# A bias copied into PSUM by ScalarE, border rows packed into tiles that run on demand, and new order lists

## The chip, the core and the metric

The kernel runs on one core of a Trainium2 chip. It is one program with five instruction queues: TensorE (PE, matrix products into PSUM), VectorE (DVE), ScalarE (ACT), GpSimd (POOL, which also issues the indirect DMAs) and SyncE (SP, which issues the other DMAs). Each queue runs in order; semaphores join them. The metric is device microseconds of one execution.

## What is computed

The input x has 16 x 512 = 8192 rows (tokens) of 512 float32 values. Each token has a pathway id (0 to 499), an id c (0 to 4) and a mask m (0 or 1, used as an index into a table of three).

```python
h = _ln(x, pw_g[pathway_ids], pw_b[pathway_ids])
h = _ln(h, cp_g[compartment_ids], cp_b[compartment_ids])
t = _ln(x, tm_g[time_steps], tm_b[time_steps])
m = x + _mlp_ln(memory_state, ...)[:, None, :]
n = x + _mlp_ln(noise_state, ...)[:, None, :]
r = x + _mlp_ln(resource_state, ...)[:, None, :]
s = _ln(x, ms_g[scale_type], ms_b[scale_type])
w = jax.nn.softmax(aw)
cat = jnp.concatenate([w[0]*h, w[1]*t, w[2]*m, w[3]*n, w[4]*r, w[5]*s], axis=-1)
return _mlp_ln(cat, int_W1, int_b1, int_W2, int_b2, int_g, int_be)
```

Here `_ln` is a layer norm over the 512 values with a row's own gain and offset, and `_mlp_ln` is a first layer, silu, a second layer and a layer norm. The output is x plus the returned rows. compartment_ids and time_steps are both c, and scale_type is m.

## The kernel before

**Sorting.** t and s depend on a token only through x, c and m. So the kernel first sorts the 8192 tokens by their pair (c, m), 15 groups in a snake order (NG = 15, B = 16 batches), and works through 64 tiles of 128 sorted rows, four to a window, 16 windows. Within a tile of one group the gains of t and s can be folded into the weights: `s_part` (ACT, line 247) and `build` (DVE, line 255) make the matrix `vs` of a group, and only where the group changes from the tile that last used that buffer.

**The border rows.** A tile through which a border between two groups runs is worked with the group of its middle row. The rows on the other side of the border (at most 64 a border) need a correction, and the kernel works these out first as extra tiles: before, one tile for the borders at which m changes, and six in which each half (64 rows) belongs to one of two neighbouring borders of c (NX = 6, lines 1043 to 1313). An extra tile gathers its rows of x (`gx.e`), takes their sums and norm (`xs.e`, `nv.e`), gathers the difference of the two groups' gains (`gr`), multiplies (`mt`, line 1274), transposes on TensorE (`ey`, line 1281), copies out (`ez`, line 1288), multiplies by the weights (`ex`, line 1296), gathers and adds a row of the bias table (`ea`, `ee`) and is written to a table in DRAM by SP (`eo`, lines 1309 and 1313). The gathers are always issued. The steps on TensorE, VectorE and ScalarE stand behind a condition, `some[k] > 0`, which says that a border of the tile isn't at the edge of a tile. Later each tile of the main loop gathers one row of that table per token (`ga`, line 165) and adds it to its first layer.

**The main loop.** For each tile the first layer is the sum of three products: x with the weight block X, the normed x with `vs` (V, line 394), and h with block H. X and H of two tiles and two column halves go through a seven-product scheme (`m7`, line 442, 128x256 products). Then come the add (`ha`, line 462), the silu (`hs`, ACT, line 465), a transpose in 32x32 blocks on VectorE (`tz`, line 191) and 16 DMAs on SP (`sZ`, line 199) which finish the transpose. GpSimd makes the sums that the second layer's seven-product scheme needs (`zs`, lines 522 to 528), and TensorE runs it (`q7`, line 545), for window w - 1 while window w's first layer is at work. Each pair of tiles has two PSUM banks for it, `pq_pa` and `pq_pb`; there are eight banks in all. The second layer's bias enters as a product: before products 1 and 5 of each pair, TensorE multiplies a constant with the bias, which `bias_parts` has split into three bf16 parts (line 543, 96x128 with 96x256). ScalarE and VectorE copy and add the halves out of PSUM (`kf`, `ku`, `sf`, `sl`, lines 554 to 574). The last window's second layer is an ordinary product (`l2`, line 477), with its bias added by VectorE (line 605).

**Order.** The program text is three lists of short names. ORDER is the preparation, the extra tiles and window 0's first layer; WINDOW is run for w = 0 to 14, where c, p, n and m stand for windows w, w - 1, w + 1 and w + 2; LAST is the last window. Each name calls a function through the tables at lines 1360 to 1384, and each engine gets its instructions in the order of the list. A queue that waits holds back what stands behind it.

## Time and profile before

| | |
|---|---|
| median of 3 runs | 937.35 us (935.75 to 942.13) |
| the profiled execution | 936.66 us |
| its span, first to last instruction | 934.8 us |
| mean granted TensorE clock | 0.991 |

The profile names an instruction by its line, engine, what it writes and reads, and its shape. A float32 product counts as two records. Busy time of TensorE is that of pipelined instructions, whose own durations overlap: the step from one start to the next is what a product costs in a dense stretch. The chain of work that ended last is followed back from the end, and its pieces don't overlap. In a table by stretches the columns are the length, then for each engine its busy time and number of instructions, then the granted clock, the busy share of the DMA engines and GB/s. A wait's row gives what waited, on what, the total, how often, and the longest.

### The profile page before, as it was taken

Reading aid. Unit: us, or ns where it says so; the run is one execution under the profiler, and the core shown is the slowest. Engines: PE = TensorE matmul, PEld = TensorE weight load, DVE = VectorE, ACT = ScalarE, POOL = GpSimd, SP = SyncE. Lnnn points to the kernel's source line nnn. Section 1 sums busy time; section 2 is a strip of 40 time slices with the busy share of each in tenths; the row PEclk is TensorE's granted clock in tenths of the full one; section 3 lists DMA queues with packets and bytes.
Section 4 is the critical chain, followed back from the end, with each engine's and each line's share of the span. In section 5 each row is a group of like instructions: output and inputs, shape, how many; then the busy total and the mean of one; then the engine's idle time right before and its main releaser. Section 6 shows DMA issues by size and latency. Waiting matters only on the chain. (4 is left out here: it accounts for less than half of the span.)

```text
span 934.8 us, 13620 instructions
## 1 busy us (share of the span) xinstructions
PE 898.4 (96%) x3687; PEld 644.4 (69%) x3687; DVE 746.1 (80%) x1359; ACT 500.9 (54%) x1211; POOL 662.1 (71%) x705
## 2 busy tenths in 40 slices
PE   6979999999999999999999999999999999999995
PEld 6644447868677677878576776778686867777782
DVE  8678677969688798979687886959798987979475
ACT  4688646264635638373645446273747465472322
POOL 9666787767777687687677677767867776875523
PEclk9899999999999999999999999999999999999998
DMA  8667686776767686777767685857767676866512
GB/s 282 215 241 224 206 255 163 213 209 184 235 176 236 171 243 162 226 198 206 212 174 232 183 241 155 250 157 229 205 200 218 182 224 176 249 171 185 166 40 95
DMA packets 88860, 186.66 MB, mean 200 GB/s; under 512 B 24372, under 2 KB 24372, under 8 KB 88780
## 3 DMA queue, kind: packets, MB, share of 16 engines
q0 software_dynamic: 31376, 106.19, 38.8%
q1 hardware_dynamic: 56700, 79.50, 29.5%
q8 instruction: 30, 0.49, 0.2%
q14 instruction: 50, 0.41, 0.1%
q10 hardware_dynamic: 704, 0.08, 0.1%
HBM read 101.78 MB, written 19.94 MB: 130 GB/s over the span
## 5 line engine op out<-in xcount | busy, mean ns | idle before, releaser
L394 PE MATMUL p<-vs,catV 128*128 128x512 f32 x512 | 227.7, 592 | 1.7 <-DVE vs L255 1.5
L394 PEld LDWEIGHTS p<-vs,catV 128*128 128x128 f32 x512 | 97.0, 190 | 106.0 <-issue 97.1
L340 ACT ACTIVATE junk<-pw 128x512 bf16<-128x512 f32 x60 | 37.8, 630 | 170.7 <-DVE pw L337 162.2
L636 POOL DMA_INDIRECT out<-yb,tok x64 | 72.1, 1126 | 57.3 <-DVE yb L632 25.3
L442 PE MATMUL p<-wh__80,catH 128*128 128x256 f32 x480 | 110.9, 379 | 0.0
L442 PEld LDWEIGHTS p<-wh__80,catH 128*128 128x128 f32 x480 | 91.2, 190 | 18.4 <-issue 6.7
L362 POOL TENSOR_TENSOR rsh<-veh,mhalf 128x1 f32<-128x1 f32 x64 | 55.8, 872 | 42.3 <-DVE veh L358 37.1
L165 POOL DMA_INDIRECT pw<-in_pw,i_pw x64 | 66.1, 1032 | 26.9 <-DVE rH L191 9.2
L381 POOL TENSOR_TENSOR xbs<-xbs,rows 128x512 f32<-128x512 f32 x64 | 81.9, 1281 | 1.0
L165 POOL DMA_INDIRECT xbs<-in_x,tok x64 | 66.6, 1041 | 22.2 <-issue 16.5
L165 POOL DMA_INDIRECT cp<-cp_rows,i_cp x64 | 67.6, 1056 | 17.3 <-issue 14.4
L366 ACT ACTIVATE pw<-pw,rsh 128x512 f32<-128x512 f32 x64 | 45.8, 719 | 63.0 <-DVEq L238 43.0
L165 POOL DMA_INDIRECT add<-rows,i_add x64 | 66.9, 1045 | 16.4 <-issue 11.0
L465 ACT ACTIVATE add<-add 128x512 f32<-128x512 f32 x64 | 40.3, 632 | 70.0 <-DVE add L462 67.6
L307 ACT ACTIVATE xm<-xbs,nmx,rsx 128x512 f32<-128x512 f32 x64 | 49.1, 809 | 26.8 <-DVE nmx L301 25.7
L442 PE MATMUL p<-wt,catH 128*128 128x256 f32 x240 | 56.7, 379 | 0.0
L442 PE MATMUL u<-wt,catX 128*128 128x256 f32 x240 | 56.6, 379 | 0.0
L442 PE MATMUL u<-wx__79,ss 128*128 128x256 f32 x240 | 56.5, 379 | 0.0
L191 DVE STREAM_TRANSPOSE rH<-pw 128x512 f32<-128x512 f32 x60 | 41.0, 701 | 18.6 <-ACT pw L366 16.6
L337 DVE SCALAR_TENSOR_TENSOR pw<-pw,rsx 128x512 f32<-128x512 f32 x64 | 53.0, 829 | 2.3
L442 PE MATMUL u<-wt,ss 128*128 128x256 f32 x240 | 54.4, 379 | 0.0
L442 PE MATMUL u<-wx__79,catX 128*128 128x256 f32 x240 | 54.4, 379 | 0.0
(421 smaller groups left out, 2097.9 us busy)
## 6 DMA issues: line engine op xcount, KB each, us to landing
catX<-rX SPq DMA_DIRECT2D x240, 64.0 KB
catV<-rV SPq DMA_DIRECT2D x240, 64.0 KB
catZ<-rZ SPq DMA_DIRECT2D x240, 64.0 KB
catH<-rH SPq DMA_DIRECT2D x240, 64.0 KB
rows<-adde SPq DMA_DIRECT2D x14, 128.0 KB
yb<-in_int_W SPq DMA_DIRECT2D x1, 1024.0 KB
catH<-in_int_W SPq DMA_DIRECT2D x1, 1024.0 KB
w1x<-in_int_W SPq DMA_DIRECT2D x1, 1024.0 KB
```

Source lines behind the costliest of these rows:

```text
L165: nc.gpsimd.indirect_dma_start(dst, None, table, bass.IndirectOffsetOnAxis(ap=idx, axis=0), **kw)
L191: nc.vector.transpose(rot[:, :, :, j, :].rearrange("p q c t -> p c q t"), src.rearrange("p (c q t) -> p c q t", c=NC, q=Q))
L307: nc.scalar.activation(t, st["xb"][:, j, :], AF.Identity, bias=st["nm"][:, j : j + 1], scale=st["rs"][:, j : j + 1])
L337: nc.vector.scalar_tensor_tensor(h, h, st["rs"][:, j : j + 1], pw[:, D:], ALU.mult, ALU.add)
L340: nc.scalar.activation(junk, x, AF.Identity, accum_out=sums[:, 0, k : k + 1])
L362: nc.gpsimd.tensor_tensor(rs, st.pop(("ve", j)), mhalf[:, :1], ALU.pow)
L366: nc.scalar.mul(pw[:, :D], pw[:, :D], st.pop(("rs", j)))
L381: nc.gpsimd.tensor_add(st["xb"][:, j, :], st["xb"][:, j, :], rows[:, 2, :])
L394: nc.tensor.matmul(st["p1", g], st["c" + blk][:, g, c, :], m[:, c, :], start=(blk == first and c == order[0]), stop=(blk == last and c == ...
L442: nc.tensor.matmul(dst, m[:, c], at_["half1"][k][:, c], start=(k == 1 and c == 0), stop=(c == NC - 1), skip_group_check=True)
L465: nc.scalar.activation(st["add", g], st["add", g], AF.Silu)
L636: nc.gpsimd.indirect_dma_start(out_rows[j], bass.IndirectOffsetOnAxis(ap=tok[:, j, w : w + 1], axis=0), yb[:, j, :], None)
```

## The change

1. **The second layer's bias.** The bias products and the three bf16 parts go. `rows` becomes a view of `blocks`, seven half rows, the last of them zero; `bias_parts` only subtracts one half from the other. Two new pieces fill a bank before its products, which then all accumulate: `kb` (`put_bias`) is one ScalarE copy of 128x512 into the bank, [bias half, zeros], in windows 1 to 14, four a window; `kz` (`clear_sums`) is a product of zeros that does the same clearing once in window 0. `weights_back` restores the bias for the last window.
2. **The border rows.** Every border's rows that need work are counted (`count_ends`), and added up in front of each other (`row_places`), so that they fill up to seven full tiles without gaps (NT_ = 7). The tile of m borders takes 64 rows for each of its two borders. Which token a packed row is comes from products with a comparison matrix (`of_begins`, `kinds`) and a new gather of one value a row from the sorted list, which is now also written to DRAM (`in_order`, `gt`). A tile runs when the total reaches it. The gathers of tokens, of x and of the differences now stand behind that condition too, on GpSimd; the gathers of bias rows don't. Each tile is written by one DMA of SP, not two.
3. **The lists.** ORDER, WINDOW and LAST are new throughout. In WINDOW, V's fourth tile (`lV.c.3`) now comes ahead of the first product of Z, and its third (`lV.c.2`) ahead of the last two. In ORDER, the blocks of x's weights (`wk`) are all summed before the first variance (`xe.0`), and the transposes of x come first. In LAST, the last `sh` stands ahead of `po.c.0`, where it stood behind `po.c.1`.

The diff, cut to its core:

```diff
 WINDOW = """
-    ha.p.2 sh.c.1 lV.c.1 lV.c.0 m7.c.0.1 m7.c.1.1 hs.p.2 tz.p.3 tz.p.2 f1.c.2 sp.c.3 fs.c.2 f1.c.3 xs.n.0 fs.c.3
-    gc.c.2 gc.c.3 ga.c.0 sh.c.0 bd.c.3 fv.c.2 f2.c.2 fv.c.3 f2.c.3 sZ.p.0 sZ.p.1 sZ.p.2 sZ.p.3 sp.c.2 q7.p.0.1
-    q7.p.0.2 lV.c.3 fp.c.2 fp.c.3 zs.p.0 fn.c.2 fn.c.3 xs.n.1 xs.n.2 kf.p.0 bd.c.2 th.c.3 th.c.2 zs.p.1 q7.p.1.1
-    q7.p.0.5 q7.p.0.7 xs.n.3 tx.n.3 sf.p.0 tx.n.1 tx.n.0 xe.n gh.n.0 zs.p.2 q7.p.0.6 zs.p.4 zs.p.5 zs.p.3 xp.n
-    q7.p.1.2 kf.p.1 ku.p.0 sf.p.1 vd.n tx.n.2 sl.p.0 r1.c.0 xm.n gc.n.1 zs.p.6 zs.p.7 sh.c.3 q7.p.1.5 q7.p.0.3
-    q7.p.1.7 q7.p.0.4 kf.p.2 nv.n.3 nv.n.1 kf.p.3 sf.p.2 tv.n.3 tv.n.1 sf.p.3 sl.p.1 nv.n.2 nv.n.0 lq.p.0 ga.c.2
-    gc.n.0 ga.c.1 gh.n.1 sH.c.1 sH.c.3 sH.c.0 sH.c.2 q7.p.1.6 q7.p.1.3 q7.p.1.4 lV.c.2 m7.c.1.2 lq.p.1 ku.p.1
...
+    kz.p.2 kz.p.1 ha.p.2 f1.c.2 kb.p.2 kz.p.0 ga.c.2 tz.p.3 lV.c.1 lV.c.0 m7.c.1.1 m7.c.0.1 kb.p.1 sh.c.1 kb.p.0
+    gc.c.2 gc.c.3 sp.c.3 hs.p.2 tz.p.2 bd.c.3 f1.c.3 fs.c.2 sp.c.2 xs.n.0 fs.c.3 fv.c.2 bd.c.2 f2.c.2 fv.c.3
+    f2.c.3 sZ.p.0 sZ.p.1 sZ.p.2 fp.c.2 ga.c.0 zs.p.0 fp.c.3 lV.c.3 q7.p.0.1 q7.p.0.2 q7.p.0.7 xs.n.1 fn.c.2 fn.c.3
+    kf.p.0 xs.n.2 zs.p.1 zs.p.2 q7.p.0.5 q7.p.0.6 ku.p.0 kf.p.1 tx.n.1 th.c.2 th.c.3 tx.n.3 r1.c.0 sZ.p.3 gh.n.0
+    zs.p.3 zs.p.4 sf.p.0 tx.n.2 sf.p.1 zs.p.5 xs.n.3 zs.p.6 q7.p.1.2 vd.n tx.n.0 r1.c.1 xe.n xp.n ga.c.1 ga.c.3
+    sH.c.3 sh.c.2 zs.p.7 sH.c.2 kz.p.3 q7.p.1.1 sl.p.0 sH.c.0 sH.c.1 q7.p.0.3 q7.p.0.4 kb.p.3 kf.p.2 va.n sf.p.2
+    sl.p.1 xm.n q7.p.1.5 q7.p.1.7 nv.n.1 nv.n.3 lq.p.0 kf.p.3 f1.n.0 tv.n.3 tv.n.1 sf.p.3 q7.p.1.6 lV.c.2 q7.p.1.4
...
@@ -207,7 +213,11 @@
     def gather_x(st, js=range(NJ)):
         t, w = st["tok"]
         for j in js:
-            gather(st["xb"][:, j, :], x_rows, t[:, j, w : w + 1])
+            if "n" in st:
+                with tc.If(at_["some", 3][int(st["w"][1]) * Q + j] > 0):
+                    gather(st["xb"][:, j, :], x_rows, t[:, j, w : w + 1])
+            else:
+                gather(st["xb"][:, j, :], x_rows, t[:, j, w : w + 1])
 
     def gather_h(st, j):
...
     def weights_back():
         nc.gpsimd.tensor_add(w2[:, :2, D // 2 :], w2[:, :2, D // 2 :], w2[:, :2, : D // 2])
+        nc.gpsimd.tensor_add(blocks[:, 1], blocks[:, 1], blocks[:, 0])
 
     def bias_parts():
-        BF16 = mybir.dt.bfloat16
         H = D // 2
-        parts = 96
...
+        nc.gpsimd.memset(blocks[:, 6], 0.0)
+        nc.vector.tensor_sub(blocks[:, 1], blocks[:, 1], blocks[:, 0])
+
+    def clear_sums(st, i):
+
+        if st["w"] == 0:
+            st["pq", i] = psum(f"pq0_{i // 2}{'ab'[i % 2]}").rearrange("p (k n) -> p k n", k=2)
+            zero = blocks[:, 6].bitcast(mybir.dt.bfloat16)
+            nc.tensor.matmul(st["pq", i].rearrange("p k n -> p (k n)"), zero[:, :P], zero, start=True, stop=True,
+                             skip_group_check=True)
+
+    def put_bias(st, i):
+        if st["w"]:
+            st["pq", i] = psum(f"pq{st['w']}_{i // 2}{'ab'[i % 2]}").rearrange("p (k n) -> p k n", k=2)
+        nc.scalar.copy(st["pq", i], blocks[:, 1::5] if i % 2 else blocks[:, 0::6])
 
...
     def seventh(st, p, k):
-        ab, ed = sums_of(st, p)
-        home = {1: ab[:, 0], 6: ab[:, 0], 2: ab[:, 1], 5: ed[:, 0], 3: ed[:, 0], 7: ed[:, 1], 4: ed[:, 1]}[k]
+        i, half = {1: (0, 0), 6: (0, 0), 2: (0, 1), 5: (1, 0), 3: (1, 0), 7: (1, 1), 4: (1, 1)}[k]
         if ("zp", p) not in st:
             st["zp", p] = {1: st["cZ"][:, 2 * p, :2], 2: st["cZ"][:, 2 * p, 2:]}
-        bias = at_["bias"]
-        if k in bias:
-            nc.tensor.matmul(home, at_["share"], bias[k], start=True, stop=False, skip_group_check=True)
         for c in range(2):
-            nc.tensor.matmul(home, st["zp", p][k][:, c], at_["half"][k][:, c], start=False, stop=(c == 1),
-                             skip_group_check=True)
+            nc.tensor.matmul(st["pq", 2 * p + i][:, half], st["zp", p][k][:, c], at_["half"][k][:, c], start=False,
+                             stop=(c == 1), skip_group_check=True)
 
...
+    def count_ends():
+        nc.vector.tensor_tensor(nn, dd, bf[:, 1:], ALU.min)
+        pl.tensor_mul(nn, nn, side)
+        pl.tensor_add(n_b, nn[:, :1], nn[:, 1:])
+
+    def row_places():
+        poff = psum("poff")
+        nc.tensor.matmul(poff[:NB, :1], below[:NB, :NB], n_b, start=True, stop=True)
+        nc.tensor.matmul(poff[:1, 1:2], n_b, ones[:NB, :1], start=True, stop=True)
+        nc.scalar.copy(off, poff[:NB, :1])
...
+    def segment_ends():
+        nc.vector.tensor_tensor(of_seg[:, 3:], m2[:, :1], m2[:, 1:], ALU.not_equal)
+        nc.vector.tensor_tensor(t2[:, :1], m2[:, :1], m2[:, 1:], ALU.min)
+
...
+    def segment_steps():
+        pst = psum("pst")
+        nc.tensor.matmul(pst[:NB, :4], step_1, of_seg, start=True, stop=True)
+        nc.scalar.copy(steps, pst[:NB, :4])
+
+    def list_steps():
+        pl.tensor_scalar(lists, lists, off, None, ALU.is_ge)
 
...
     nc.tensor.matmul(idle[:, : 3 * P], wt[:, 0, :P], wt[:, 0, : 3 * P], start=True, stop=True)
+    nc.sync.dma_start(in_order.rearrange("(k r) o -> k (r o)", r=P), at_c)
     i_w = by_place(ident[: Q * NW, : Q * NW])
...
     def of_begins():
 
...
+        at_["pnx"] = pnx = ps.tile([P, NE, 4], F32, tag="p", name="pnx")
+        nc.tensor.matmul(pnx[:, 0], at_border.rearrange("p v n -> p (v n)"), of_s, start=True, stop=True)
+        for j in range(NT_):
+            nc.tensor.matmul(pnx[:, 1 + j], lists[:, j * P : (j + 1) * P], steps, start=True, stop=True)
...
     def extras_flags():
-        nc.vector.tensor_copy(some[:1, : NX + 1], at_["pf"][:1, : NX + 1])
+
+        two = prep.tile([P, 2], I32, name="two")[:1]
+        nc.vector.tensor_copy(two, row_beg[:1, NR5 - 1 :: NR5][:, :2])
+        nc.vector.tensor_scalar(two, two, P - 1, None, ALU.bitwise_and)
+        nc.vector.tensor_add(some[:1, :1], two[:, :1], two[:, 1:])
+        nc.vector.tensor_scalar(some[:1, 1:NE], i_ext[:1, 1:NE], total[:1], None, ALU.is_lt)
 
...
+    def gather_token(e, j):
+
+        k = e * Q + j
+        with tc.If(at_["some", 3][k] > 0):
+            gather(tokf[:, k : k + 1], in_order[:, :], pos_x[:, k : k + 1])
+
+    def tokens_of(e):
+        at = slice(e * Q, (e + 1) * Q)
+        nc.vector.tensor_copy(add_x[:, at], tokf[:, at])
+        nc.vector.tensor_scalar(tok_x[:, at], add_x[:, at], PW, None, ALU.logical_shift_right)
+
+    def rows_of(e):
+        at = slice(e * Q, (e + 1) * Q)
+        b = f_x[:, 3, at]
+        nc.vector.tensor_scalar(add_x[:, at], add_x[:, at], S.bit_length() - 1 + PW, None, ALU.logical_shift_right)
+        nc.vector.tensor_copy(b, add_x[:, at])
+        t = f_x[:, 0, at]
+        nc.vector.tensor_sub(t, f_x[:, 1, at], b)
+        nc.vector.tensor_mul(t, t, e_x[:, at, 3])
+        nc.vector.tensor_add(t, t, b)
+        nc.vector.tensor_add(add_x[:, at], t, e_x[:, at, 2])
 
...
     def gather_diff(st, j):
         k = int(st["w"][1]) * Q + j
         st["r", j] = r = gp.tile([P, D], F32, tag="cp", name=f"pr{st['w']}_{j}")
-        gather(r, diff_rows[:, :], tok_x[:, 1, k : k + 1])
+        with tc.If(at_["some", 3][k] > 0):
+            gather(r, diff_rows[:, :], diff_x[:, k : k + 1])
 
...
     def extra_out(k):
-        if k == 0:
-            nc.sync.dma_start(rows_1[NB1:, :], at_["adde", k])
-        H = P // 2
-        at = [b for b in range(NB) if (b % NR5 == NR5 - 1) == (k == 0)][2 * max(k - 1, 0) :]
-        for v in range(2):
-            nc.sync.dma_start(rows_2[NB1 + at[v] * H : NB1 + (at[v] + 1) * H, :], at_["adde", k][v * H : (v + 1) * H])
+        to, at = (rows_1, 0) if k == 0 else (rows_2, k - 1)
+        nc.sync.dma_start(to[NB1 + at * P : NB1 + (at + 1) * P, :], at_["adde", k])
 
```

408 lines of the change are left out of this document (199 added, 209 removed).

## The prediction

> **What bounds the kernel now.** I read the page first, then TensorE's waits, the chain that ended last, and two periods of the main loop.
>
> ```profile
> span 934.8 us, 13620 instructions
> PE 898.4 (96%) x3687; PEld 644.4 (69%) x3687; DVE 746.1 (80%) x1359; ACT 500.9 (54%) x1211; POOL 662.1 (71%) x705
> ```
> ```profile
> PE pc L810 <- DVE sm L816: 6.9, 1, 6.9
> PE pq_1b L545 <- POOL catZ L524: 4.5, 6, 1.5
> PE pq_0a L545 <- DMA catZ<-rZ: 4.1, 8, 1.2
> ```
> ```profile
> 715.37:767.45 52.08, 50.86 (x205) 37.99 (x205) 45.49 (x83) 29.81 (x72) 38.41 (x39) 1.00 0.72 206
> 767.45:819.63 52.18, 51.25 (x204) 37.81 (x205) 43.69 (x76) 28.68 (x69) 37.78 (x39) 1.00 0.72 202
> ```
> ```profile
> 715.37 1.97 PE pq_0a L545 x8
> 717.34 3.43 PE p L394 x8
> 720.77 0.11 PE pq_1a L543
> 720.88 0.87 PE pq_1a L545 x4
> ...
> 754.06 7.31 DMA catX<-rX
> ```
>
> TensorE is busy 96% of the span, and in the two periods 50.86 of 52.08 us and 51.25 of 52.18 us, at full clock. From 715.37 to 754.06 the chain runs through TensorE alone, each piece beginning where the last one ended. So the main loop costs what TensorE has to do plus what it waits for: 4.1 us in 8 places for the first tile of Z (the transposed hidden rows of the window before) and 4.5 us in 6 places for GpSimd's sums of Z. The 6.9 us is the start, the same in both kernels. A piece taken from TensorE's list in the loop is worth its whole distance in the chain, provided that what it waits for next comes in time.
>
> **A. The bias products.** The chain gives one bias product 0.11 us (720.77 to 720.88), not the 0.27 us of its own pipelined duration.
>
> ```profile
> 0.00:935.00 935.00, 16.45 (x60) 5.86 (x60) 0.99 0.69 200
> ```
>
> That is line 543 over the span: 60 of them, 60 x 0.11 = 6.6 us. The changed kernel instead has 4 zero products in the first window (512 columns where the bias has 256, so 0.22 us each, 0.9 us). Net **-5.7 us**, all on TensorE's path.
>
> **B. The copies into PSUM.** Each of the other 14 windows gets four ScalarE copies of 128x512 from SBUF into PSUM, 56 in all. No row of the trace writes PSUM from ScalarE. The nearest are these:
>
> ```profile
> L340 ACT ACTIVATE junk<-pw 128x512 bf16<-128x512 f32 x60 | 37.8, 630 | 170.7 <-DVE pw L337 162.2 <-ACT yb L567 7.8 <-ACT junk L342 0.3
> L1135 ACT COPY ev<-po 128x512 f32<-128x512 f32 x3 | 1.8, 588 | 2.9 <-PE po L1131 2.9
> L307 ACT ACTIVATE xm<-xbs,nmx,rsx 128x512 f32<-128x512 f32 x64 | 49.1, 809 | 26.8 <-DVE nmx L301 25.7 <-ACT junk L342 0.7
> ```
>
> I take 0.63 us, the same shape with one read from SBUF; the ends are 0.59 (reading PSUM) and 0.81. ScalarE is busy 29 of 52 us in a period, so 4 x 0.63 = 2.5 us of it costs nothing in itself. What it can cost is delay at two places, worked out in C. It cannot save anything there, since ScalarE loses no work for it.
>
> **C. The new order in the loop.** The product of V's fourth tile now stands ahead of the first product of Z, not behind the second. These rows show one approach to Z:
>
> ```profile
> 704.70 6.60 PE L394 MATMUL p<-vs,catV 128*128 128x512 f32 x15
> 714.60 0.27 PE L543 MATMUL pq_0a<-b2r,ident 96*128 96x256 bf16 x1
> 715.37 1.97 PE L545 MATMUL pq_0a<-w,catZ 128*128 128x256 f32 x8 [0.50 <-DMA catZ<-rZ]
> 767.45 1.97 PE L545 MATMUL pq_0a<-w,catZ 128*128 128x256 f32 x8 [1.22 <-DMA catZ<-rZ]
> ```
> ```profile
> 707.62 0.63 ACT L465 ACTIVATE add<-add 128x512 f32<-128x512 f32 x1 [0.56 <-DVE add L462]
> 707.51 1.49 DVE L191 STREAM_TRANSPOSE rZ<-add 128x512 f32<-128x512 f32 x2
> 709.07 10.02 SPq L199 DMA_DIRECT2D catZ<-rZ  x16
> ```
>
> Count from V's first product at 704.70. The last silu ends at 3.6 us, its transpose at 4.3, SP's issues begin at 4.4, and Z is there at 10.7 (the other period: some 11.8). TensorE reaches Z after 6.87 us of V and 3.45 us of half products, at 10.3. With V's fourth tile in front it arrives at 10.3 + 3.43 = 13.75.
>
> Three copies (kb.p.2, kb.p.1, kb.p.0) now stand on ScalarE ahead of the last silu (hs.p.2), 1.9 us; 0.56 us of it lies in the wait that the silu has today, so Z comes some 1.3 us later, at about 12 to 13.1. A front_1 of 1.45 us put ahead of the transposes on VectorE lies beside those copies. TensorE's wait for Z should go, with 0.7 to 1.7 us to spare; if the cover were gone, each window would pay what Z is late beyond 13.75. The sums of Z on GpSimd start when Z lands, as now, while their first reader stands later on TensorE: 9 products of 0.86 us behind Z's first, at 21.5, where it stood at about 20.5. Of the 4.5 us little should be left.
>
> The fourth copy (kb.p.3) is the risk. It takes a bank that pq_0a leaves (eight banks, all in use then), and ScalarE has the copy-out of pq_0a and of pq_0b (0.37 each) and a row-sum group in front of it:
>
> ```profile
> 718.61 0.61 ACT L340 ACTIVATE junk<-xbs 128x512 bf16<-128x512 f32 x1
> 720.21 0.19 ACT L342 ACTIVATION_READ_ACCUMULATOR junk<-xbs,sums 128x1 f32 x1
> ```
>
> The group takes 718.61 to 720.40, 1.8 us. From the end of product 6 of the first pair to the first product that needs the new bank TensorE has four products, 3.45 us; ScalarE needs 0.37 + 0.37 + 1.8 + 0.63 = 3.2 us and its semaphores. The margin is 0.2 us or less, with what is queued behind TensorE's next product waiting too. At 0.81 a copy the margin is nothing. I take 0.2 us a window in 14 windows, 3 us, between 0 and 0.5 a window. C: -8.6 + 3.0 = **-5.6 us**.
>
> **D. The border rows.** Now one tile for style borders and six for pairs of other borders; a tile runs when one of its borders isn't at a tile's edge:
>
> ```profile
> 0.00:935.00 935.00, 17.92 (x40) 7.44 (x40) 0.99 0.69 200
> 0.00:935.00 935.00, 3.02 (x20) 2.22 (x20) 0.99 0.69 200
> ```
>
> Line 1296 (products) has 40 records at eight a tile, line 1281 (transposes) 20 at four: five tiles ran, 3.58 + 0.60 = 4.2 us each on TensorE. Counted from the reference's inputs, the nine real borders lie 37, 123, 54, 51, 90, 47, 15, 100 and 69 rows into their tiles, so the packed lists hold 37 + 5 + 54 + 51 + 38 + 47 + 15 + 28 + 59 = 334 rows: three full tiles and the halved one. Four run where five ran, and the stage behind 72 us is TensorE's: **-4.2 us**. The fifth tile's sums, scaling and add on ScalarE and VectorE, the six bias-splitting steps around 120 to 127 us, and 7 of 15 writes of these rows on SP go too. I count them at nothing, beside TensorE's products.
>
> **E. The preparation up to 130 us.**
>
> ```profile
> 50.00:60.00 10.00, 5.01 (x42) 2.43 (x35) 7.07 (x19) 8.36 (x23) 6.24 (x7) 0.91 0.96 370
> 60.00:70.00 10.00, 9.01 (x59) 5.15 (x58) 7.93 (x30) 9.29 (x17) 6.62 (x7) 0.92 0.27 87
> ```
> ```profile
> 70.32 0.75 DVE L1112 SCALAR_TENSOR_TENSOR wx__79<-w1x,wx,wx__79 128x512 f32<-128x512 f32 x1
> 72.24 3.60 PE L394 MATMUL p<-wx__79,catX 128*128 128x512 f32 x8
> 43.39 1.52 POOL L165 DMA_INDIRECT xbs<-in_x,tok_x  x1 [2.18 <-issue]
> 45.21 0.95 POOL L165 DMA_INDIRECT xbs<-in_x,tok_x  x1 [0.30 <-PE pa L982]
> 69.99 1.29 PE L1281 MATMUL px<-ident,pre 128*128 128x128 f32 x8
> 112.04 3.69 PE L1296 MATMUL pe<-wt,catX 128*128 128x512 f32 x8 [0.32 <-PEq L1279]
> ```
>
> Today the last weight block of x is summed at 70.32 and the first window's products start at 72.24, behind 6 us of TensorE idle between 50 and 70. The new list sums all eight blocks before the first variance, so two of those products can fill that hole: at most -6. Against it, the first border gather, at 43.39 now, needs more: steps on GpSimd, one product, another, some ten short VectorE steps, then four token gathers at 1.25 us (0.95 and 0.30 between two) on a queue that held 21 gathers and now holds 20 and 24 conditions (0.3 us each by the one row, 0 to 8 us). I get the first border transpose at 71 to 72 us, where it is at 70 now, and TensorE there at 67 to 71. Ends: -6 and +10. I take **-1.0**, near the two 1.0 us apart that this walk gives, and not the middle, since the hole is measured and the delay is not.
>
> **F. The tail.**
>
> ```profile
> 922.17 0.68 DVE L582 TENSOR_TENSOR yg<-yb,rows 128x512 f32<-128x512 f32 x1
> 925.00 1.82 DVE L582 TENSOR_TENSOR yg<-yb,rows 128x512 f32<-128x512 f32 x1
> 924.99 1.27 POOL L381 TENSOR_TENSOR xbs<-xbs,rows 128x512 f32<-128x512 f32 x1
> ```
>
> GpSimd's last shift of x runs beside VectorE's scaling, which takes 1.82 us where its twin took 0.68. The new list has that shift earlier: **-1.1 us**, or 0 if it meets another.
>
> **Sum:** -5.7 - 5.6 - 4.2 - 1.0 - 1.1 = -17.6 us. The profiled execution took 936.66 us (934.8 of span and 1.9 around it), so 919.1; the median of the runs is 0.7 above it: 937.35 - 17.6 = **919.8 us**.
>
> **The rivals.**
> *R1, the hole is filled and nothing new waits.* E gives its -6 and C none of its +3: 919.8 - 5 - 3 = 912. For it: ScalarE's 54%. Against: the margin of 0.2 us.
> *R2, the border lists come late.* TensorE is in order and stands at the first border transpose until the rows are there. At +10 in E: 919.8 + 11 = 931, within 1% of before. For it: the longer chain on GpSimd. Against: by the walk in E the two come within 1 to 4 us of each other. The Trainium skill ("TensorE: Matmul & The Clock Gate", What's actually happening) has the clock fall to half after some 3.4 us of idling and stay there until as long a busy stretch; by that an estimated 1.7 us comes on top, 933. The trace bears it out about as far: 0.91 and 0.92 in the two stretches around the 5 us hole.
> *R3, TensorE isn't the limit.* VectorE is busy 80% and the window's loop runs through it; if the loop is VectorE's, the period stays near 52 us and only what VectorE loses counts: one tile's multiply and add (two operations like the 0.68 us one in F, 1.4 us) and a dozen short list steps, at most 5 us together: 932. Against: TensorE's gapless chain. The Trainium skill ("Perfetto Trace Analysis", Identifying the Most-Contended Engine) calls matmul busy time a bad measure and goes by weight loading, here 69%, which puts VectorE first; the gapless chain speaks against it.
> *R4, slower: the copies hold ScalarE.* If the three copies ahead of the last silu wait for banks, the silu, its transpose, 16 issues on SP and Z wait behind them. Nothing is lost up to 13.75 us; past it each microsecond costs 14. At 17.6/14 = 1.3 us beyond (Z at 15.0) the whole gain is gone; with Z at 16.4 it makes 919.8 + 14 x 2.65 = 957. Against: I count five of eight banks held when the copies come.
>
> **How the numbers follow.** Forecast 0.56, R1 0.14, R2 0.14, R3 0.06, R4 0.10. Predicted is the forecast's time. 1% (9.4 us) is about what a measurement of this kernel tells from no change: faster means under 928. Faster has the forecast, R1 and 0.04 of R2: 0.74. Within 1% are 0.10 of R2, R3, and 0.04 of R4 with Z only a little late: 0.20. Slower has the rest of R4: 0.06. The range, 909 to 932, reaches from R1's side with 3 us more for copies at 0.59 and a shorter end, to R2 and R3; left out are half of R1's low side, the clock's part of R2 and most of R4, 0.2 together.
>
> **What would show it.** A: no line 543 and 60 fewer short products. C: a period of 50.3 to 50.5 us, no wait of pq_0a for Z's DMA, GpSimd waits under 1 us in sum; if kb.p.3 is late, pq_1b waits for ScalarE's copy. D: 32 records of border products and 16 transposes. E: the first x product near 54 us, and the first border transpose near 71. F: no 1.8 us scaling at the end. Wrong would be: a period that stays near 52, TensorE waiting for ScalarE by a microsecond a window, or a main loop that starts no earlier than today.

## The result, and the profile after

The changed kernel took 934.01 us (median of 17 runs, 927.09 to 937.33), the kernel before 938.4 us in the 17 runs beside it: a ratio of 0.9932, interval 0.9906 to 0.9957. That is 0.7% faster, inside the 1% that was to count as no change, which the prediction gave a chance of 0.20, and 2 us above the top of the predicted range. The same kernel was timed on two more chips in the study, as e5 and e10: 930.68 us, 0.985 [0.9811, 0.9889], and 931.99 us, 0.9913 [0.9882, 0.9944]. So it is faster on all three, by 4 to 14 us, and nowhere by the 17.6 us that the sum gave. (Each ratio here is against runs of the kernel before on the same chip.)

The profiled execution of the changed kernel took 930.14 us. The page's span and engine shares, and then TensorE's waits (what waited, on what, total, times, longest):

```profile
span 928.4 us, 13749 instructions
PE 892.2 (96%) x3617; PEld 642.1 (69%) x3617; DVE 735.6 (79%) x1360; ACT 521.2 (56%) x1261; POOL 651.7 (70%) x730
```
```profile
PE pc L810 <- DVE sm L818: 7.2, 1, 7.2
PE px L1350 <- DVE pre L1343: 3.4, 1, 3.4
PE ptH L1201 <- ACT pw L376: 3.1, 2, 2.2
PE pq_0b L546 <- DVE yb L565: 2.5, 12, 0.2
PE pq_0b L546 <- POOL yb L532: 2.1, 4, 0.8
```

Both waits of the main loop that the prediction set out from are gone from the list, that for Z's DMA (4.1 us in 8 places) and that of pq_1b for GpSimd's sums (4.5 us in 6). The second row is new: 3.4 us in one place, at a border transpose, in the preparation. New too are the last two rows, waits of the loop at another bank: pq_0b waits for VectorE's add and, in 4 places, for GpSimd's sums. Two periods of the loop, an early and a late one (length, each engine's busy time and instructions, clock, DMA share, GB/s):

```profile
204.91:255.35 50.44, 50.23 (x202) 37.91 (x201) 41.22 (x74) 28.54 (x70) 36.55 (x38) 1.00 0.74 208
660.85:712.82 51.97, 50.91 (x201) 37.64 (x200) 44.79 (x81) 31.02 (x73) 37.13 (x38) 1.00 0.72 199
```

The early one is TensorE's without a gap worth the name: 50.23 of 50.44 us. In the late one VectorE builds `vs` anew for two groups, and TensorE loses 1 us to waits. The early one is called undisturbed below: it comes back to within 0.02 us in seven of the loop's 14 periods in each of the three profiles of the changed kernel.

To see where the time went, the span is cut at two marks that both kernels have, the first V product of window 1 and that of window 15. From TensorE's timeline, of the kernel before and then of the changed one (start, duration, instruction):

```profile
136.56 7.03 PE L394 MATMUL p<-vs,catV 128*128 128x512 f32 x16
859.91 7.03 PE L394 MATMUL p<-vs,catV 128*128 128x512 f32 x16
```
```profile
59.38 3.70 PE L404 MATMUL p<-wx__80,catX 128*128 128x512 f32 x8
...
77.86 0.63 PE L1350 MATMUL px<-ident,pre 128*128 128x128 f32 x4 [1.36 <-issue]
...
140.71 7.03 PE L404 MATMUL p<-vs,catV 128*128 128x512 f32 x16
...
853.87 1.45 PE L404 MATMUL p<-vs,catV 128*128 128x512 f32 x3
```

With the second profile of the kernel before (e9) and the two further ones of the changed kernel (e5, e10), read in the same way:

| us | first x product | first mark | first to second mark | second mark to end | span |
|---|---|---|---|---|---|
| before | 72.24 | 136.56 | 723.35 | 74.89 | 934.8 |
| before, e9 | 73.34 | 137.38 | 727.82 | 74.80 | 940.0 |
| changed | 59.38 | 140.71 | 713.16 | 74.53 | 928.4 |
| changed, e5 | 62.51 | 141.95 | 717.92 | 74.43 | 934.3 |
| changed, e10 | 58.63 | 139.48 | 714.95 | 74.47 | 928.9 |
| means, changed less before | -12.6 | **+3.7** | **-10.2** | -0.4 | -6.9 |

The loop gained 10.2 us where parts A and C together had -12.2 (-6.6 for the bias products in the loop, -5.6 for the order). The tail gained 0.4 us. The rest was lost ahead of the first mark: the x products start 12.6 us sooner, and yet the main loop starts 3.7 us later. Profiles of one kernel differ by up to 4.8 us in the loop and by 2.5 us at the first mark, but in every pairing of these rows the loop is shorter in the changed kernel (by 5.4 us at least) and the first mark later (by 2.1 at least). (For the first mark e5 had 140 to 142 us expected and e10 140.7 to 142: the one came as expected, the other 1.2 us sooner.)

### The profile page after: what moved, and what is told of

Same layout as the page of the kernel before. It is cut to its first block, busy times and chain, and to the rows that moved or that the text cites. A ratio compares the mean times of both kernels' runs of the same rounds, so it can differ in the third digit from the quotient of the medians.

```text
span 928.4 us, 13749 instructions
## 1 busy us (share of the span) xinstructions
PE 892.2 (96%) x3617; PEld 642.1 (69%) x3617; DVE 735.6 (79%) x1360; ACT 521.2 (56%) x1261; POOL 651.7 (70%) x730
## 5 line engine op out<-in xcount | busy, mean ns | idle before, releaser
L638 POOL DMA_INDIRECT out<-yb,tok x64 | 66.5, 1039 | 31.6 <-issue 17.9
L171 POOL DMA_INDIRECT pw<-in_pw,i_pw x64 | 64.2, 1003 | 26.0 <-DVE rH L197 12.8
L171 POOL DMA_INDIRECT add<-rows,i_add x64 | 69.2, 1082 | 15.6 <-issue 15.6
L383 DVE SCALAR_TENSOR_TENSOR pw<-pw,sumsh,cp 128x512 f32<-128x512 f32 x60 | 43.9, 753 | 43.8 <-DMA cp<-cp_rows,i_cp 43.6
L346 DVE SCALAR_TENSOR_TENSOR pw<-xbs,sums,pw 128x512 f32<-128x512 f32 x60 | 59.9, 998 | 13.7 <-DMA pw<-in_pw,i_pw 11.2
L625 POOL TENSOR_TENSOR rsy<-vey,mhalf 128x4 f32<-128x4 f32 (+1 forms) x16 | 21.6, 1348 | 64.4 <-DVE vey L620 64.4
L612 ACT ACTIVATE junk<-yb 128x512 bf16<-128x512 f32 x64 | 40.2, 628 | 38.2 <-DVE yb L576 27.9
L452 PE MATMUL u<-wt,ss 128*128 128x256 f32 x240 | 56.7, 379 | 0.0
```

The lines of the kernel that those rows point to most:

```text
L171: nc.gpsimd.indirect_dma_start(dst, None, table, bass.IndirectOffsetOnAxis(ap=idx, axis=0), **kw)
L346: nc.vector.scalar_tensor_tensor(h, st["xb"][:, j, :], st["sums"][:, 1, j : j + 1], h, ALU.add, ALU.mult)
L383: nc.vector.scalar_tensor_tensor(pw[:, :D], pw[:, :D], st["sh", j][:, 1], cp, ALU.add, ALU.mult)
L452: nc.tensor.matmul(dst, m[:, c], at_["half1"][k][:, c], start=(k == 1 and c == 0), stop=(c == NC - 1), skip_group_check=True)
L612: nc.scalar.activation(junk, yb[:, j, :], AF.Square, accum_out=st["ssy"][:, j : j + 1])
L638: nc.gpsimd.indirect_dma_start(out_rows[j], bass.IndirectOffsetOnAxis(ap=tok[:, j, w : w + 1], axis=0), yb[:, j, :], None)
```

## The experiments

**What holds up the preparation.** The list that the prediction walked through had a step that it did not count: `lw`, the load of the second layer's weights on SP (1 MB), stood ahead of the border rows and now stands behind one of their writes. SP's timeline before and after:

```profile
48.39 0.38 SPq L1350 DMA_DIRECT2D w<-in_int_W  x1
```
```profile
81.58 0.40 SPq L1404 DMA_DIRECT2D w<-in_int_W  x1
```

Three theories: (1) the load now falls among the gathers of the border rows and delays them; (2) the variance of x and ScalarE's place in the new list make the border rows late; (3) the added gather of tokens does. e1 moves the load alone:

```diff
-... ct fs.0.2 do xs.e0.0 ... wb ro.0 lw sp.0.0
+... ct fs.0.2 do lw xs.e0.0 ... wb ro.0 sp.0.0
```

> The changed kernel with one name moved in ORDER: the load of the second layer's weights (1 MB, issued by SyncE at 81.58 us, behind the two writes of the bias table) goes back to where the kernel before has it, right behind the write of the gain differences (about 50 us). Theory 1, the load collides with the gathers: VectorE's wait for a gather of gains (4.93 us at 92.88), the wait of GpSimd for border tile 0's row (3.97 us) and TensorE's wait for the third border tile (3.36 us) shrink, the first product of V of window 1 comes 3 to 6 us earlier than 140.71, the time falls by as much. Theory 2, x's variance stands too late behind the border list, and theory 3, the second gather makes the border lists late: nothing of these moves, the time stays within 1 us.

It took 929.64 us, 0.9894 [0.9854, 0.9933]. Measured from the first x product, which takes the clock of the first 60 us out of it, the first mark comes at 75.26 us, against 81.33, 79.44 and 80.85 in the three profiles of the changed kernel. The stretch where the load now lies, first in the changed kernel, then in e1:

```profile
80.00:90.00 10.00, 10.00 (x33) 4.93 (x32) 5.67 (x13) 9.25 (x15) 5.46 (x7) 1.00 0.94 305
90.00:100.00 10.00, 5.79 (x18) 2.99 (x17) 6.70 (x10) 4.83 (x13) 4.61 (x6) 0.83 0.67 213
```
```profile
80.00:90.00 10.00, 10.00 (x34) 5.01 (x33) 7.00 (x14) 9.12 (x16) 5.89 (x7) 1.00 0.75 256
90.00:100.00 10.00, 8.50 (x26) 3.98 (x25) 7.07 (x15) 8.28 (x23) 8.28 (x8) 1.00 0.69 213
```

From 80 to 90 us the DMA engines are busy 94% with the load and 75% without it, and ten microseconds later TensorE has 5.79 us of work against 8.50. Between the two lies this, in the timeline of the changed kernel (in brackets the wait before, and on what):

```profile
81.58 0.40 SPq L1404 DMA_DIRECT2D w<-in_int_W  x1
...
82.63 0.95 POOL L171 DMA_INDIRECT cp<-cp_rows,i_cp  x1 [0.83 <-PE ptH L1201]
...
92.88 0.75 DVE L381 SCALAR_TENSOR_TENSOR pw<-pw,sumsh,cp 128x512 f32<-128x512 f32 x1 [4.93 <-DMA cp<-cp_rows,i_cp]
...
98.59 1.11 PE L1350 MATMUL px<-ident,pre 128*128 128x128 f32 x4 [3.36 <-DVE pre L1343]
99.50 5.55 PE L1365 MATMUL pe<-wt,catZ 128*128 128x512 f32 x8
99.91 1.02 POOL L171 DMA_INDIRECT adde<-rows,i_x  x1 [3.97 <-DMA rows<-adde]
```

and in that of e1:

```profile
50.29 0.38 SPq L1404 DMA_DIRECT2D w<-in_int_W  x1
...
88.20 0.75 DVE L381 SCALAR_TENSOR_TENSOR pw<-pw,sumsh,cp 128x512 f32<-128x512 f32 x1 [1.42 <-DMA cp<-cp_rows,i_cp]
...
94.67 0.66 PE L1350 MATMUL px<-ident,pre 128*128 128x128 f32 x4 [1.08 <-DVE pre L1343]
95.17 3.65 PE L1365 MATMUL pe<-wt,catZ 128*128 128x512 f32 x8
```

A gather of one row per token is issued a microsecond behind the load. VectorE stands 4.93 us for it (1.42 without the load), and what is queued behind that step, the multiply of the fourth border tile, reaches TensorE 3.36 us late (1.08). The wait costs twice: in 90 to 100 us the granted clock is 0.83, and the tile's transposes and products take 1.11 and 5.55 us, against 0.66 and 3.65 at full clock. The Trainium skill ("TensorE: Matmul & The Clock Gate", What's actually happening) has the clock halved after an idle window of some 3.4 us; this trace agrees as far as a mean can show it, with a wait of 3.36 us and 0.83 over the ten microseconds around it. The Trainium skill ("DMA: Bandwidth & Descriptors", SWDGE vs HWDGE vs iDMA) also says that GpSimd's DMAs and SP's are carried out by the same engines, which agrees with a load on SP delaying a gather on GpSimd.

e11 repeats e1 beside the unchanged kernel (e10) on one chip.

> The changed kernel with the load of the second layer's weights issued early, once more, now beside the changed kernel itself. Theory 1: the first product of V of window 1 comes 5 to 7 us earlier than in the changed kernel, as the first time (134.47 against 140.71), and the time is 4 to 7 us under it. Rival, that difference was chance: within 1.5 us.

> The changed kernel as it is, beside the next two. Expected as in its two profiles: first product of V of window 1 at 140.7 to 142, loop 716 to 722 us.

e11: 927.92 us, 0.9869 [0.9824, 0.9914]; first mark 75.84 us behind the first x product, where e10 has 80.85. (By the clock of the trace it comes 3.5 us sooner, where 5 to 7 were expected, since e11's first x product is 1.5 us later than e10's.) The waits named above are 0.6, 1.6 and none, against 3.5, 4.2 and 4.0 us in e10. By profile theory 1 holds, for 5.0 us (means 80.5 and 75.55); the timed gain of 4.1 us has the same size, though its intervals overlap.

e4 is the counterpart: in the kernel before, the load moved behind the writes of the bias table.

```diff
-... gx.1.2 lw ro.0 ro.1 ex.0
+... gx.1.2 ro.0 ro.1 lw ex.0
```

> The kernel before with one name moved: the load of the second layer's weights behind both writes of the bias table on SyncE, so from 48.39 to about 75 us, as the changed kernel has it. Theory 1: gathers that land behind 75 us come up to 5 us later, the first product of V of window 1 comes 2 to 6 us later than 136.56, and the time rises by as much. Theories 2 and 3: within 1 us of the kernel before; it may even fall, since the stretch of 50 to 58 us in which TensorE waits for a load loses its competitor.

0.9994 [0.9974, 1.0015]. The load was issued at 72.80 us, the first mark lies 66.59 us behind the first x product (64.32 and 64.04 before), and that product comes 1.5 to 2.6 us sooner, while the DMA share of 50 to 60 us falls from 0.96 to 0.71. So in the old list the late load costs about 2.4 us in one place and about as much comes back in another; the rise of 2 to 6 us that theory 1 expected here did not come. That the load costs by what it meets, and not by being late as such, fits both lists, but for the old one it is argued and not shown: the granted clock of the first stages, too, differs between these profiles.

**The other two theories.** e2 puts the variance of x ahead of the step `kd`, e3 takes the gather of tokens away, e14 does the same on top of e1.

```diff
-... xv.0.0 kd xs.0.0 xs.0.2 wk.2.2 cg wk.2.0 xe.0 ... gh.0.2 xp.0
+... xv.0.0 xs.0.0 xs.0.2 xe.0 kd xp.0 wk.2.2 cg wk.2.0 ... gh.0.2
```

> The changed kernel with x's last two row statistics and its variance ahead of the border list on VectorE, and x's power ahead of the token gathers on GpSimd. Theory 2: the norms of x on ScalarE start at about 55 and not at 61.08, the sums of the border rows follow sooner, the first border transpose comes at 74 to 75 and not 77.86, the first product of V of window 1 2 to 4 us earlier than 140.71. Theory 3: the token gathers come 1 us later, and so does the first border transpose (79); time +1 us. Theory 1: the first stages move but what TensorE waits for behind 90 us does not; time within 1 us.

```diff
 def gather_token(e, j):
-    with tc.If(at_["some", 3][k] > 0):
-        gather(tokf[:, k : k + 1], in_order[:, :], pos_x[:, k : k + 1])
+    return
...
-    nc.vector.tensor_scalar(tok_x[:, at], add_x[:, at], PW, None, ALU.logical_shift_right)
+    nc.vector.tensor_copy(tok_x[:, at], pos_x[:, at])
```

> The changed kernel without the gather that looks up which token a packed border row is: the place in the sorted list is used as the token's number, so other rows are corrected, as many and in the same tiles. Theory 3: the border rows of x are gathered 6 us earlier (at about 56, not 62.03), the first border transpose comes at 71 to 72, and the time falls by 5 to 7 us. Theory 2: ScalarE is occupied up to 66 us whatever the gathers do; the first border transpose comes at most 1.5 us earlier and the time falls by 0 to 1.5 us. Theory 1: the same small number, since the waits behind 85 us stay.

> The early load, and the token's number taken from the place without the gather, so other rows are corrected, as many and in the same tiles. With the load out of the way theory 3 is tested alone: if the second gather is what leaves the first border transpose at 77 to 78.5 us, it comes 4 to 6 us earlier, and the stretch from the first product of x to the first product of V of window 1 falls from 75.5 to 71 or 72. If the norms of x and the sums on ScalarE set it, the first border transpose stays within 1.5 us and the stretch within 1.5 us of 75.5.

e2: 0.9926 [0.9901, 0.9952], with the first border transpose 18.3 us behind the first x product, as in the changed kernel (18.3 to 18.5). e3: 0.9926 [0.989, 0.9963], transpose 19.2 us behind, so no sooner; its first mark does come 4.4 us sooner than in the changed kernel's profile, by smaller waits behind 85 us. With the load early there is nothing left of that: e14 has its mark 76.65 us behind the first x product, where e1 and e11 have 75.26 and 75.84 (0.9847 [0.9772, 0.9922], a wide interval). Theory 3 falls as the cause of the late border transpose, and theory 2 in this form. e17 and e18 tried theory 2 further, on e1: the sums, the variance and the power of x ahead of `kd` and its scaled mean right behind it (e17), and the variance and power of the border rows earlier as well (e18).

> The changed kernel with the early load, and x's last two statistics, variance, power and scaled mean all ahead of the conditioning rows and the token gathers (the earlier try moved the variance but left the scaled mean behind them, and ScalarE's norms began no sooner against the first product of x). Theory 2: the norms of x begin 1.5 us or more sooner against the first product of x (1.70 us behind it in the first profile of the changed kernel), the first border transpose follows (18.4 us behind it so far, then 16 to 17), and the stretch from the first product of x to the first product of V of window 1 falls from 75.5 to 73 to 74. Rival, the border rows of x land at 64 us and the sums can't start before: the first border transpose stays at 18 to 18.5 and the stretch at 75 to 76.

> As the one before, and the border rows' variance on VectorE ahead of a product that waits for a gather of gains, their power on GpSimd ahead of the next gather. If what stands between the sums' end and the first border transpose (4.5 us) holds queues that wait for something else, the first border transpose comes 1 to 1.5 us sooner than in the one before and so does the first product of V of window 1. Rival, TensorE's order has other waits behind it that take up the slack: within 0.5 us of the one before.

Both made it later, with the transpose 23.0 and 25.8 us behind the first x product: 0.9938 [0.9912, 0.9964] and 0.997 [0.9942, 0.9997]. In ScalarE's timeline of e17 the third and fourth norm of x wait 9.37 us for a product on TensorE, which they do not in e1:

```profile
71.04 1.59 ACT L317 ACTIVATE xm<-xbs,nmx,rsx 128x512 f32<-128x512 f32 x2 [9.37 <-PE p L404]
```

The sums of the border rows, next on ScalarE, then begin 10.7 us behind the first x product, where they begin 6.7 us behind it in e1. So the edit brought a wait of its own, and whether the norms of x hold the border rows back is left open by it.

e12 goes the other way. It gives TensorE more to do while the border rows come, on e1: `vv.0.3 vv.0.0` ahead of `nv.e0.0`, and the V product `lV.0.1` ahead of `ey.0`.

> As the one before, and in ORDER window 0's product of V's second tile stands ahead of the first border transpose, and the two copies of normed x that it needs ahead of the border rows' norms on ScalarE. Then TensorE has 3.4 us of work where it waits for the border rows at 72 to 78 us. If it is the border rows' lateness that leaves the rest of the loss: 1.5 to 2.5 us earlier at the first product of V of window 1 than with the early load alone (about 132.3). If the border rows are the limit all through the stage, what runs in that hole only pushes them back: 0, or up to 1 us later.

926.73 us, 0.9851 [0.9805, 0.9898], the lowest median of the study. But the mark lies 75.44 us behind the first x product, no sooner than in e1 and e11: the first border transpose comes 2 us later, pushed back by the product that is now ahead of it, and the gain of 1.2 us over e11 is not one that can be told. What the first mark follows is the fourth border transpose: it comes 39.6 to 40.1 us behind it in all six kernels with the early load and four tiles (e1, e11, e12, e14, e17, e18), wherever the first transpose stands, and 41.4 to 42.1 behind it in the three profiles of the changed kernel. Work pulled into the wait for the first tile doesn't shorten this stage; what sets its end is when the last of these rows come.

**What a border tile is worth.** e13 runs a fifth tile, on e1, by comparing the total with a tile's index less one.

```diff
-    nc.vector.tensor_scalar(some[:1, 1:NE], i_ext[:1, 1:NE], total[:1], None, ALU.is_lt)
+    nc.vector.tensor_scalar(some[:1, 1:NE], i_ext[:1, : NE - 1], total[:1], None, ALU.is_lt)
```

> The changed kernel with the load of the second layer's weights issued early and one border tile more: the condition of tile k takes the limit of tile k - 1, so five tiles run where four did; the fifth works rows that no token fetches. My term D: a tile is worth its 12 instructions on TensorE, 4.2 us at the first product of V of window 1 counted from the first product of x (75.3 and 75.8 us in the two profiles without it, so 79.7), and as much time. Rival, TensorE waits for the border rows there anyway and the tile fits into the waits: under 1.5 us. Rival, the fifth tile comes late too and TensorE waits for it: 6 us or more.

0.9968 [0.9932, 1.0004], where e14, timed on the same chip with four tiles, has 0.9847. The first mark moves by 11.8 us against the mean of e1 and e11 (87.36 behind the first x product), where a tile's products and transposes are 4.2 us. A wait of ScalarE (85 to 125 us) and two of TensorE (60 to 125 us):

```profile
ACT junk L350 <- DMA xbs<-in_x,i_x: 4.8, 1, 4.8
```
```profile
PE ptH L1201 <- ACTq L286: 4.4, 1, 4.4
PE ptH L1201 <- ACT pw L376: 2.4, 1, 2.4
```

The fifth tile opens the second group of tiles. Its gather comes when ScalarE is already due to sum it, ScalarE stands, and TensorE stands behind ScalarE. So in the new list this tile, the first of the second group, is worth more than its products; what the tile that went saved in the old list was not measured by itself.

**What the loop gained by.** e6 puts 60 short products of zeros back where the bias products stood, e5 is the unchanged kernel beside it.

```diff
+        if k in (1, 5):
+            zero = blocks[:, 6].bitcast(mybir.dt.bfloat16)
+            nc.tensor.matmul(st["pq", 2 * p + i][:, half], zero[:96, :P], zero[:96, : D // 2], start=False, stop=False, ...)
         for c in range(2):
```

> The changed kernel with 60 more short products on TensorE, 96x128 with 96x256 in bf16 like the bias products of before and at their places, but with zeros, so that the sums stay. My term A: each costs 0.11 us, 6.6 us in all, and every undisturbed period of the loop grows from 50.44 to 50.88. Rival, a product costs what its record shows (0.27 us): 16 us, 51.5 a period. Rival, they lie in waits that the loop has anyway: under 2 us.

> The changed kernel as it is, once more, for what a second profile of the same kernel shows. If the waits behind 85 us are the kernel's own and not chance, the first product of V of window 1 comes at 140 to 142 us again (140.71 in the first profile), the waits of VectorE for a gather of gains (4.93) and of GpSimd for border tile 0's row (3.97) are there again, and the loop from the first product of Z to that of window 15 takes 714 to 721 us (716.6).

0.9915 [0.988, 0.995] against 0.985 [0.9811, 0.9889]. The loop is 720.29 us, 5.0 more than the mean of the three profiles without them (715.3) and 2.4 more than in e5, the one from the same chip. The undisturbed windows tell more. Z's first product starts twice in these rows of TensorE's timeline of e6, with one of the later short products between:

```profile
206.24 0.27 PE L547 MATMUL pq_0a<-rows 96*128 96x256 bf16 x1
206.35 1.89 PE L549 MATMUL pq_0a<-w,catZ 128*128 128x256 f32 x8
...
210.78 1.03 PE L549 MATMUL pq_1a<-w,catZ 128*128 128x256 f32 x4
211.65 0.27 PE L547 MATMUL pq_1a<-rows 96*128 96x256 bf16 x1
...
212.88 1.10 PE L549 MATMUL pq_0b<-w,yb 128*128 128x256 f32 x4
...
257.13 1.89 PE L549 MATMUL pq_0a<-w,catZ 128*128 128x256 f32 x8
```

and the same place in the changed kernel:

```profile
209.22 1.89 PE L546 MATMUL pq_1a<-w,catZ 128*128 128x256 f32 x8
211.32 1.10 PE L546 MATMUL pq_0b<-w,yb 128*128 128x256 f32 x4 [0.21 <-DVE yb L565]
```

206.35 to 257.13 is 50.78 us, against 50.44 (204.91 to 255.35): four short products lengthen a window by 0.34 us, though the step from the start of each to the next product's is 0.11 or 0.12. The third of the four adds nothing. From the first product of pq_1a to that of pq_0b with `yb` it is 2.10 us in both kernels (210.78 to 212.88, 209.22 to 211.32), because in the changed kernel pq_0b waits there for VectorE's add, and in e6 the short product lies in that wait. So a short product costs its 0.11 us where TensorE has no wait, and three of four a window count. e16 asks for the same in the old list: the kernel before, its bias products left out.

```diff
-        if k in bias:
-            nc.tensor.matmul(home, at_["share"], bias[k], start=True, stop=False, skip_group_check=True)
         for c in range(2):
-            nc.tensor.matmul(home, st["zp", p][k][:, c], at_["half"][k][:, c], start=False, stop=(c == 1), ...)
+            nc.tensor.matmul(home, st["zp", p][k][:, c], at_["half"][k][:, c], start=(k in bias and c == 0), ...)
```

> The kernel before without the bias products; the second layer's bias is left out in 15 of 16 windows. My term A: 6.6 us less (60 x 0.11), the loop 722 to 726 where two profiles have 728.5 and 732.9. Rival, in the old order TensorE then only reaches its waits for Z earlier: those grow from 4 to 8 us and the time falls by under 2.5 us.

> The kernel before as it is, for a second profile of it beside the other kernels of this set. If only the chip is slower here, its loop and its preparation both grow by less than 1 us against the first profile (first product of V of window 1 at 136.56, loop 728.5 us). If it is sensitive to late DMAs in the loop, its waits for Z grow beyond 4.1 us and the loop beyond 731.

No gain that shows: 0.9992 [0.9953, 1.0031], from 4.4 us less to 2.9 more (e9, the kernel before against itself, has 0.998), and a loop of 730.58 us, not below the 723.35 and 727.82 of the kernel before. In TensorE's waits of e16 the time is there again; below its two largest rows stands the one that e9 has for Z's DMA:

```profile
PE pq_0a L543 <- DMA catZ<-rZ: 8.4, 11, 1.3
...
PE pq_0a L543 <- DVE yb L559: 4.9, 4, 1.5
```
```profile
PE pq_0a L545 <- DMA catZ<-rZ: 7.7, 11, 1.6
```

The wait for Z's DMA alone doesn't tell, since the kernel before has 4.1 us of it in one profile and 7.7 in the other. But all waits ahead of the second layer's products come to 21.7 us in e16, against 8.6 and 13.5 there. With 6.6 us less to do TensorE comes to these products sooner and waits for them longer. Leaving out the bias products showed its worth only with the order that takes those waits away. That order was taken apart by two kernels: e7 is the changed kernel with V's fourth tile back behind the second product of Z, e8 the kernel before with it ahead of the first.

```diff
-... fp.c.3 lV.c.3 q7.p.0.1 q7.p.0.2 q7.p.0.7
+... fp.c.3 q7.p.0.1 q7.p.0.2 lV.c.3 q7.p.0.7
```
```diff
-... sp.c.2 q7.p.0.1 q7.p.0.2 lV.c.3 fp.c.2
+... sp.c.2 lV.c.3 q7.p.0.1 q7.p.0.2 fp.c.2
```

> The changed kernel with the product of V's fourth tile moved back in WINDOW, from ahead of the first product of Z to behind the second. My term C: the waits for Z come back, and the loop grows by about 8.6 us (4.1 for Z's DMA, 4.5 for GpSimd's sums), more since Z is later than before by the three copies ahead of the silu: up to 14 x 1.3 = 18 us. Rival, the rest of the new WINDOW brings Z sooner than I counted: under 3 us.

> The kernel before with one name moved in WINDOW: the product of V's fourth tile ahead of the first product of Z. My term C: both waits go, 8.6 us of the loop, the first product of Z comes 3.4 us later in a window and finds its data; 929 where the kernel before takes 938. Rival, the waits only move (TensorE then waits for GpSimd's sums or for a bank later in the window): 0 to 4 us.

e7: 0.9959 [0.9931, 0.9986] against 0.985 on the same chip, 942.29 us against 930.68, and a loop of 727.87 us, 12.5 more than the changed kernel's mean. e8: 1.0033 [1.0, 1.0065], between nothing and 6 us slower. (Its profile has a loop of 739.55 us, 14 more than the mean of the kernel before, but it is of one of e8's longer runs, 953.66 us, and the kernel before was profiled on other chips; e7's is of its longest.) Their waits, e7 and then e8:

```profile
PE pq_0a L546 <- ACT sumsh L351: 5.5, 2, 2.9
...
PE pq_0a L546 <- issue: 3.6, 2, 3.2
```
```profile
PE pq_0a L545 <- POOL catZ L524: 6.3, 4, 1.6
PE pq_0a L545 <- DVE yb L561: 5.9, 4, 2.8
PE p L394 <- DVE veh L358: 5.4, 3, 2.5
```

In e7 TensorE stands at Z's first product again, though not in every window: five of the 14 periods are within 0.1 us of the undisturbed 50.44, and the last four hold most of the loss (223.1 us, against 210.2 to 214.8). Only 1.7 us of the waits there are put down to Z's DMA, so which of Z's inputs is late is not settled. In e8, where that move alone was made, TensorE waits at least as long, for GpSimd, VectorE and V's own inputs, which nothing had moved to fit. The one move is worth 11.6 us in the new list and nothing in the old one, or a small loss.

e15 does the fourth copy into PSUM (`kb.p.3`) twice, which the prediction had as the risk.

```diff
-        nc.scalar.copy(st["pq", i], blocks[:, 1::5] if i % 2 else blocks[:, 0::6])
+        for _ in range(2 if i == 3 else 1):
+            nc.scalar.copy(st["pq", i], blocks[:, 1::5] if i % 2 else blocks[:, 0::6])
```

> The changed kernel with the fourth copy into PSUM (the one into the bank that the first pair leaves) made twice, 0.63 us more on ScalarE in 14 windows. My term C has that copy late by 0.2 us a window: then all of the second copy is on TensorE's path, 14 x 0.63 = 8.8 us, and an undisturbed period is 51.07 and not 50.44. Rival, the copy has a margin (no product waits for it in the profile): the period stays at 50.44 and the time within 1 us.

0.9876 [0.9801, 0.9952]. The undisturbed period stays at 50.44 us, so another 0.58 us on ScalarE at that place is hidden there. The loop as a whole has 721.19 us in a profile of its longest run, 5.8 above the mean and 3.3 above the longest of the unchanged kernel; the excess lies in the disturbed windows, where no row of TensorE's waits in the loop names ScalarE, and where it comes from was not settled.

## Why the prediction was off, by its own steps

**What failed is E, with D.** The prediction counted D at -4.2 and E at -1.0, and put the zero products at +0.9, most of it ahead of the first mark (three of the four, 0.22 us each by their starts, 0.65). Measured up to that mark is +3.7, so D and E together are +3.1 and not -5.2, off by 8.3 us. One of the prediction's own signs of being wrong, a main loop that starts no earlier than today, is what came. Three things were wrong in that step:

- *A moved transfer was not counted.* E followed the gathers on GpSimd's queue and left SP's out. The load that went from 48.39 to 81.58 us makes 5.0 of the 8.3 us, shown by e1 and e11.
- *The walk to the first border transpose was too short.* It was to be at 71 to 72 us and came at 77.86. In all three profiles it is 18.3 to 18.5 us behind the first x product, where the walk gave 17 to 18; but that product came at 58.6 to 62.5 where 54 was named. From 50 to 60 us TensorE has no gap, with other products that stand ahead of x's, at a granted clock of 0.83:

```profile
50.00:60.00 10.00, 10.00 (x66) 5.50 (x67) 8.22 (x28) 4.88 (x11) 6.47 (x7) 0.83 0.26 68
```

So the hole was filled, as E said, but not by x's products alone, and the stage ends when the border rows come. E took the -1.0 of its walk, on the ground that the hole was measured and the delay was not. That was a reason to leave it wide. The remaining 3.3 us lie in this walk: neither the token gather nor the place of x's variance accounts for them, e17 and e18 leave the norms open, and which step of the longer chain does is not known.

- *The count of D was right, its price was not its own.* There are 32 product records and 16 transposes, as said. The rows are the products over the whole span and then the transposes:

```profile
0.00:929.00 929.00, 16.42 (x32) 6.65 (x32) 0.99 0.70 200
```
```profile
0.00:929.00 929.00, 2.97 (x16) 2.05 (x16) 0.99 0.70 200
```

A tile was priced at its time on TensorE, 4.2 us. Even there the four tiles took 19.4 us, only about 1.5 less than the five of before, with the fourth at the lower clock. In a stage that waits for rows a tile is worth what it delays, 11.8 us for the fifth one in e13; in the old list it may have been worth less than 4.2. Only the sum of D and E is known.

**A, right in price, smaller in sum.** No bias product is left, and the four zero products cost what was said. By e6 the price of 0.11 us a product is right, but one of the four in a window lies in the wait for VectorE's add, so the 60 are worth 5.1 us (15 windows of 0.34) rather than 6.6. And e16 shows that the term was not free-standing: alone it had no gain that shows.

**B, right in price, off by four in the count.** There are 60 copies and not 56: the copies of window 0 are made as well, behind its products of zeros, so a bank gets its bias from ScalarE in all of the first 15 windows. They take 0.58 us, just under the low end (0.59) of what was allowed, on a ScalarE that is busy 56%. The four groups differ by 5 ns:

```profile
L520 ACT COPY pq_0a<-rows 128x512 f32<-128x512 f32 x15 | 8.7, 581 | 0.0
...
L520 ACT COPY pq_0b<-rows 128x512 f32<-128x512 f32 x15 | 8.6, 576 | 0.0
```

**C, right, with the wrong waiter.** The period was to be 50.3 to 50.5 us and is 50.44 in the undisturbed windows, no wait for Z's DMA is left, and e7 puts the worth of V's fourth tile ahead of Z at 11.6 us once the bias products are gone. The 3 us set aside for a late fourth copy were spent elsewhere: the walk had left that copy a margin of 0.2 us and then charged 0.2, and e15 hides another 0.58 there. pq_1b doesn't wait for ScalarE; pq_0b waits for VectorE's add, 0.21 us in each of 12 windows (the row shown at e6), 2.5 us in all. The waits for GpSimd's sums of Z were to fall below 1 us; they moved from pq_1b to pq_0b and are 2.1 us in 4 places. With A's smaller sum these rows are more than enough for the 2 us between -12.2 and -10.2.

**F, mostly wrong.** The prediction allowed 0 for the case that the shift meets another operation, and that case came. The last shift of x was moved out of the way, and another shift beside it now lengthens an earlier scaling:

```profile
913.28 2.29 DVE L584 TENSOR_TENSOR yg<-yb,rows 128x512 f32<-128x512 f32 x1
```

The overlap was not removed, only moved away from the last scaling; the tail gained 0.4 us of the 1.1.

**The rivals.** R2, border lists late, came nearest with 931 us and 0.14. Its mechanism was half of it: TensorE's wait at the first border transpose is only 1.36 us, because other work stood there, and the loss is in the tiles behind it; the loss of clock that R2 named came there too, 0.83 in 90 to 100 us and 1.00 in 70 to 80. R1 is out, with the lists late and pq_0b waiting. R3 is out: the period did not stay near 52, and in e6 short products on TensorE lengthened each undisturbed period by all of their time but what lies in one wait. R4 didn't come: TensorE doesn't wait for ScalarE in the loop, nor does it in e15's undisturbed windows. The low end of the range was too generous and the top too near, since the +10 of E was given weight only through one rival.

**A version that is faster still, by the profiles.** The load early on top of the change gives 929.64 us (e1) and 927.92 (e11), and 926.73 with e12's order, 1.1 to 1.5% below the kernel before. Against the changed kernel on one chip (931.99) that is 4 to 5 us less, with intervals that just overlap; the profiles show where it comes from.

## What to carry to other kernels

When a list is laid out anew, go through every queue for what moved, the bulk loads on SP above all, and ask of each which small transfers it now runs beside: one load of 1 MB among gathers cost as much as half of the loop's gain. Price a piece of work by the stage that it is in: in TensorE's nearly gapless loop three of four short products cost their full 0.11 us and the one beside a wait nothing, in a stage that waits for rows a tile of 4.2 us was worth 11.8, and work pulled into the wait was worth nothing. A saving on the busiest engine and the order that removes its waits belong together, and neither can be priced alone (no gain for the one in e16, none or a small loss for the other in e8).

## What was not expected of the hardware

The granted clock of the first 65 us differs between executions of the same kernel, 0.80 to 0.90 in 30 to 65 us for the changed one, and the first x product comes 3.9 us later with the lower one (58.63 to 62.51); for that reason the preparation was compared from that product on. The gain differs from chip to chip as well, 0.985 to 0.9932 for one pair of kernels with intervals that don't all overlap. ScalarE's copy of 128x512 from SBUF into PSUM took 0.58 us, less than the 0.63 us of the activation of the same shape over SBUF that the prediction took for it.
